# Two bottleneck blocks: filter sums in quarter pieces, eight plain products for the first two tiles, shared PSUM in the last stages

## The chip, the cores and the metric

One core of a Trainium2 chip. The metric is the device time of one execution in microseconds (us), as a median of several; the profile is one more execution under the hardware profiler. Runs of one kernel in one call differ by up to 0.4% (the kernel before: 2285.18 to 2294.29 us), and all runs used here are of the fast state.

## The reference, cut to what matters

Two blocks, one after the other, on x of 64 x 1024 x 14 x 14 (fp32). Each convolution is followed by a batch norm with the statistics of this very batch, so every stage must end before the next can scale anything.

```python
out = relu(bn(conv1x1(x,   w1, b1), g1, be1))    # 1024 -> 256 channels
out = relu(bn(conv3x3(out, w2, b2), g2, be2))    # 256 -> 256
out =      bn(conv1x1(out, w3, b3), g3, be3)     # 256 -> 1024
x   = relu(x + softplus(residual_scale) * out)
```

## The kernel before

It goes in stages, per block: conv1 (two tiles of 392 pixels at a time, seven products instead of eight, with sums of the halves on VectorE); conv2 (the 3x3 filter by transformed filters `u`, which must be computed from the taps first); the Gram stage, which transposes the normalised activations `y` and multiplies them with themselves, so that the statistics of conv3 come out without running conv3; conv3 with the residual, fused in block 0 with the next block's conv1.

The transformed filters of both blocks are built in the first stage, each half of a block's filters as one long run of VectorE instructions. Six results share two buffers, each free again only when its store to DRAM is done:

```python
def filters(b):
    for s in range(MS):
        spare = y_all[:, s, NPX // 2 - GPX :]
        ...
        for i in range(NF):
            u = part(15 * M + (i % 2) * NK * M, NK, M)         # two buffers in turn
            ...                                                # 768 elements at a time
            nc.vector.scalar_tensor_tensor(r, g[:, 1], by, base, ALU.mult, ALU.add)
            nc.vector.tensor_sub(u[:, D2], u[:, D3], u[:, D1D2])
            nc.vector.tensor_sub(u[:, D1], u[:, D0], u[:, D1D2])
            nc.gpsimd.dma_start(out=us[b][i][:, s], in_=u)
```

The weight sums for the seven products (the scheduler may move them; for the second block they landed in front of the first Gram stage):

```python
nc.vector.tensor_add(s[:, 0], a[1][0], a[1][1])
nc.vector.tensor_sub(s[:, 1], s[:, 0], a[0][0])
nc.vector.tensor_sub(s[:, 2], a[0][0], a[1][0])
nc.vector.tensor_sub(s[:, 3], a[0][1], s[:, 1])
```

The end of a Gram stage: six dense products, then the tiny ones, whose moving operand has two columns (`zmean`) or one (`ones`):

```python
for o in range(CS):
    for s in range(MS):
        nc.tensor.matmul(quad[:, o, 0:2], w3[:, s, o, :], m[:, s, :], ...)
for o in range(CS):
    for s in range(MS):
        nc.tensor.matmul(quad[:, o, 2:3], q[:, s, o * P : (o + 1) * P], ones, ...)
```

## Time and profile before

The median is 2287.72 us of 3 runs; the profiled execution has a span of 2286.1 us at a mean granted TensorE clock of 0.968 (the share of full speed that the profile shows).

| stage | from, to (us) | what to know |
|---|---|---|
| conv1, block 0, and all filters | 0 to 352.6 | five waits of TensorE for VectorE after the first load |
| conv2, block 0 | to 700.4 | 12.7 us at its start |
| Gram, block 0 | to 816.1 | 26.4 us at its start |
| statistics, conv3, residual, next conv1 | to 1469.6 | |
| conv2, block 1 | to 1817.0 | 12.7 us at its start |
| Gram, block 1, then conv3 and residual | to 2286.1 | 11 us at its start |

### The profile page before, as it was taken

The numbers are of one execution on the slowest core, as the hardware profiler recorded it, in microseconds if no ns is written. First come the engines' busy times: TensorE is split into PE (matmuls) and PEld (weight loads), VectorE is DVE, ScalarE is ACT, GpSimd is POOL, SyncE is SP. The second block draws the span as 40 slices with busy tenths as digits, with TensorE's granted clock in tenths as the row PEclk, the third lists the DMA queues.
The fourth block names the chain that finished last, engine by engine and source line by source line (L and its number), as shares of the span: only waits on it lengthen the run. The fifth ranks groups of instructions, "written<-read, shape, count | busy, mean of one in ns | idle before, by whom it ended". The sixth has DMA issues, their size and how long they took to land.

```text
span 2286.1 us, 22406 instructions
## 1 busy us (share of the span) xinstructions
PE 2164.1 (95%) x9008; PEld 1592.5 (70%) x9008; DVE 1357.5 (59%) x2086; ACT 571.0 (25%) x911; POOL 48.3 (2%) x102
## 2 busy tenths in 40 slices
PE   5989997999995999999999999799999899999997
PEld 2545556999994975555555555499999798555554
DVE  6765566887864345455555555577887633444443
ACT  1001115111113112323232232331111130444443
POOL 0000000000000000000000000000000000000000
PEclk8899998999997989999999999899999998999999
DMA  8765434555553014434434343345555410677874
GB/s 306 276 225 179 183 114 152 193 184 187 202 187 121 1 57 169 169 144 174 161 149 182 148 169 141 126 170 194 189 184 188 178 66 29 261 312 299 309 310 169
DMA packets 43016, 409.12 MB, mean 179 GB/s; under 512 B 4768, under 2 KB 5024, under 8 KB 9632
## 3 DMA queue, kind: packets, MB, share of 16 engines
q1 hardware_dynamic: 28800, 286.80, 34.4%
q0 software_dynamic: 12672, 118.49, 12.5%
q10 hardware_dynamic: 1440, 2.40, 0.3%
q8 instruction: 71, 1.16, 0.2%
q14 instruction: 33, 0.27, 0.0%
HBM read 289.18 MB, written 118.49 MB: 178 GB/s over the span
## 4 chain that ended last, share of the span: by engine, by line
PE 90%; issue 4%; DVE 2%; DMA 2%; ACT 1%; POOL 0%; ACTq 0%; POOLq 0%
PE ps L126 29%; PE bu L126 14%; PE bp L126 7%; PE ps L329 6%; PE ps L324 6%; PE ps L335 6%; PE ps L331 5%; PE ps L337 5%; PE ps L425 4%; PE bx L126 3%; PE ps L426 2%; PE ps L437 2%; DMA w<-in_w 1%; DMA u<-y 1%; PE ps L483 1%
## 5 line engine op out<-in xcount | busy, mean ns | idle before, releaser
L126 PE MATMUL ps<-y,w 128*128 128x392 f32 x2048 | 686.7, 495 | 0.6 <-DVE quad L485 0.3
L126 PEld LDWEIGHTS ps<-y,w 128*128 128x128 f32 x2048 | 391.1, 191 | 287.7 <-issue 4.4
L499 DVE SCALAR_TENSOR_TENSOR x<-ps,scale,x 128x392 f32<-128x392 f32 x512 | 317.1, 625 | 283.4 <-PE ps L126 279.1
L500 ACT ACTIVATE x<-x,shift 128x392 f32<-128x392 f32 x512 | 315.5, 622 | 442.4 <-DVE x L499 442.4
L126 PE MATMUL bu<-t,w1s 128*128 128x392 f32 x512 | 187.1, 510 | 29.4 <-DVE t L220 28.1
L357 DVE TENSOR_TENSOR f<-ps,ms 128x448 f32<-128x448 f32 x192 | 113.4, 602 | 147.2 <-PE ps L337 79.8
L324 PE MATMUL ps<-sums,u 128*128 128x224 f32 (+1 forms) x768 | 172.1, 347 | 25.4 <-DVE sums L304 12.7
L329 PE MATMUL ps<-r,u 128*128 128x224 f32 (+1 forms) x768 | 173.6, 347 | 0.0
L126 PEld LDWEIGHTS bu<-t,w1s 128*128 128x128 f32 x512 | 100.1, 197 | 105.5 <-DVE t L220 21.4
L335 PE MATMUL ps<-r,u 128*128 128x224 f32 (+1 forms) x768 | 172.1, 345 | 0.0
L324 PEld LDWEIGHTS ps<-sums,u 128*128 128x128 f32 x768 | 137.3, 190 | 26.8 <-issue 13.3
L331 PE MATMUL ps<-r,u 128*128 128x192 f32 (+1 forms) x768 | 153.8, 321 | 0.0
L337 PE MATMUL ps<-r,u 128*128 128x192 f32 (+1 forms) x768 | 153.3, 321 | 0.0
L189 ACT ACTIVATE u<-bu 128x392 f32<-128x392 f32 x96 | 47.7, 497 | 385.2 <-PE bu L126 385.2
L329 PEld LDWEIGHTS ps<-r,u 128*128 128x128 f32 x768 | 141.8, 190 | 1.3
L348 ACT ACTIVATE ms<-ps 128x448 f32<-128x448 f32 (+1 forms) x80 | 41.9, 524 | 390.7 <-PE ps L324 390.7
L335 PEld LDWEIGHTS ps<-r,u 128*128 128x128 f32 x768 | 136.0, 188 | 1.3
L439 DVE TENSOR_TENSOR zt<-ps,crow 128x512 f32<-128x512 f32 x98 | 67.8, 693 | 111.2 <-PE ps L437 111.2
L331 PEld LDWEIGHTS ps<-r,u 128*128 128x128 f32 x768 | 132.8, 189 | 1.1
L337 PEld LDWEIGHTS ps<-r,u 128*128 128x128 f32 x768 | 131.8, 188 | 1.0
L425 PE MATMUL ps<-zt 128*128 128x257 f32 x392 | 119.1, 385 | 0.5 <-DVE zt L439 0.5
L229 DVE TENSOR_TENSOR t<-x,t 128x1568 f32<-128x1568 f32 x32 | 57.3, 1792 | 84.2 <-PE bu L126 84.2
(125 smaller groups left out, 2163.3 us busy)
## 6 DMA issues: line engine op xcount, KB each, us to landing
u<-u SPq DMA_DIRECT2D x96, 1280.0 KB, 5.5
x<-in_x SPq DMA_DIRECT2D x62, 1568.0 KB, 6.6
mid<-x POOLq DMA_DIRECT2D x32, 1568.0 KB, 5.5
x<-mid SPq DMA_DIRECT2D x32, 1568.0 KB, 6.4
out<-x POOLq DMA_DIRECT2D x32, 1568.0 KB, 5.7
u<-y POOLq DMA_DIRECT2D x24, 640.0 KB, 6.9
y<-in_w SPq DMA_DIRECT2D x4, 1152.0 KB, 11.0
x<-in_x SPq DMA_DIRECT2D x4, 784.0 KB, 7.2
```

The costliest lines, as they stand in the source:

```text
L126: tc.keep_in_program_order(nc.tensor.matmul(*args, **kw))
L229: nc.vector.tensor_sub(self.v2, self.half[1][0], self.v2)
L324: nc.tensor.matmul(m[:, o, :n], w(s, D1D2), sums[:, s].rearrange("p l c -> p (l c)"), start=(s == 0), stop=(s == MS - 1),)
L329: nc.tensor.matmul(odd, w(s, D1), r[:, s, :, WH:], start=(s == 0), stop=False)
L331: nc.tensor.matmul(odd[:, :, : WH - 1], w(s, D3), r[:, s, :, WH + 1 :], start=False, stop=(s == MS - 1))
L335: nc.tensor.matmul(even, w(s, D2), r[:, s, :, :WH], start=(s == 0), stop=False)
L337: nc.tensor.matmul(even[:, :, 1:], w(s, D0), r[:, s, :, : WH - 1], start=False, stop=(s == MS - 1))
L357: nc.vector.tensor_tensor(f[:, o].rearrange("p r (i q c) -> p q (r i) c", i=GI, q=2)[:, :, :lines], eos[o][:, :, :n].rearrange("p q (l c) ...
L425: nc.tensor.matmul(g0, zt[:, c, 0:P], zt[:, c, :], start=first, stop=last)
L439: nc.vector.tensor_tensor(zt[:, :, :M], tp.rearrange("p (c m) -> p c m", c=CH), crow[:, None, :].to_broadcast([P, CH, M]), ALU.subtract,)
L499: nc.vector.scalar_tensor_tensor(v, ps, scale[:, o : o + 1], v, ALU.mult, ALU.add)
L500: nc.scalar.activation(v, v, AF.Relu, bias=shift[:, o : o + 1])
```

## The change

Its intent is to take the waits for VectorE out of the first stage and of the Gram start. The core of the diff, cut:

```diff
+        tc.keep_in_program_order(nc.vector.tensor_add(s[:, 0], a[1][0], a[1][1]))
...
+        tc.keep_in_program_order(nc.vector.tensor_sub(s[:, 2], a[0][0], a[1][0]))
...
-    def filters(b):
+    def filters(b, s, o, spare):                       # a quarter of a block's filters
+        nc.scalar.activation(even, even, AF.Copy, scale=-1.0 / 6)   # scalings to ScalarE
...
+            u = second[:, (i - 1) * n : i * n] if 0 < i < NF - 1 else first[...]   # own memory
...
+        for t, xt in enumerate(pair):
+            plain_conv1(psum, t, xt, w1[0], par[0], stats1)    # eight products, no sums
...
-            if t in (0, 6):
-                filters(t // 6)
+            if pieces and t % 4 == 2:
+                filters(0, *pieces.pop(0), spare)              # block 0, in the first stage
...
+            if k % 12 == 2 and beside:
+                beside.pop(0)()                                # block 1, in the Gram stage
...
-            with psum_pool() as psum:
+            with psum_pool(5) as psum:                         # shared with conv3 and conv1
+                made = [conv3(psum, 0, o, w3) for o in range(2)]   # ahead of the statistics
...
+            nc.vector.tensor_add(qs[0], qs[0], qs[1])          # halves the ones-products
```

The pieces in the Gram stage use the memory of the x tiles. The statistics' products are now kept in program order. PSUM stands for the buffers, called banks, that the products are written to. Not shown: the first and last term of each piece are now made by ScalarE, the two subtractions of a term are one instruction, and the four loads of a block's `w1` are issued in another order.

## The prediction

> **What bounds the kernel now.** I read the page first, then the sum of the waits of TensorE, then the order in time of the three places which that sum points at. The page says that TensorE is busy nearly all the time, and its row of slices says where it is not: slices 0 to 2 (57 us each), slice 6, slice 12, slice 25 and slice 31.
>
> ```profile
> PE 2164.1 (95%) x9008; PEld 1592.5 (70%) x9008; DVE 1357.5 (59%) x2086; ACT 571.0 (25%) x911; POOL 48.3 (2%) x102
> PE   5989997999995999999999999799999899999997
> ```
>
> The chain that ended last is 90% TensorE as well. So the time is TensorE's work plus TensorE's idle time, and a part of the change counts only if it removes one of the two. The sum of TensorE's waits gives the idle time by cause (us in total, times, longest):
>
> ```profile
> PE ps L437 <- ACT y L250: 39.1, 4, 26.4
> PE bu L126 <- DVE t L220: 28.1, 3, 12.2
> PE ps L324 <- DVE sums L304: 12.7, 1, 12.7
> PE ps L324 <- ACT t L264: 12.7, 1, 12.7
> PE bp L126 <- DVE y L198: 7.4, 2, 5.7
> PE bu L126 <- DMA w<-in_w: 7.0, 1, 7.0
> ```
>
> The L324 rows are the two starts of the 3x3 stage, which the change leaves alone. The L126 rows (42.5 us with the first load) all lie in the first stage, before 135 us. The TensorE timeline of that stretch (start, duration, then the idle time before it in brackets) shows a second cost beside each wait:
>
> ```profile
> 11.97 2.80 PE L126 MATMUL bx<-x,w 128*128 128x392 f32 x8
> 22.73 5.57 PE L126 MATMUL bu<-t,w1s 128*128 128x392 f32 x8 [7.96 <-DVE t L220]
> 56.51 5.59 PE L126 MATMUL bu<-t,w1s 128*128 128x392 f32 x8 [12.21 <-DVE t L220]
> 133.19 5.17 PE L126 MATMUL bu<-t,w1s 128*128 128x392 f32 x8 [7.91 <-DVE t L220]
> ```
>
> A product of eight instructions shows 2.80 us and follows the next after 2.63 us; after a long idle time it shows 5.2 to 5.6. VectorE is late because it builds the filters of both blocks here, in order with the sums that TensorE wants, and stands still when a filter buffer is still being stored:
>
> ```profile
> 126.11 0.96 DVE L156 SCALAR_TENSOR_TENSOR y<-y 128x768 f32<-128x768 f32 x1 [6.42 <-DMA u<-y]
> 131.35 1.78 DVE L220 TENSOR_TENSOR t<-t,x 128x1568 f32<-128x1568 f32 x1
> ```
>
> The 26.4 us wait is the start of the first Gram stage. VectorE's timeline there shows the weights of the next layer (L115, L113), which nobody needs for another 130 us, standing ahead of the few tiny instructions that make scale and shift:
>
> ```profile
> 705.65 1.89 DVE L512 BATCH_NORM_AGGREGATE mv<-stats 128x2 f32<-128x192 f32 x2
> 717.84 0.69 DVE L115 TENSOR_TENSOR w1s<-w 128x512 f32<-128x512 f32 x1 [10.31 <-DMA w<-in_w]
> 721.79 0.69 DVE L113 TENSOR_TENSOR w1s<-w 128x512 f32<-128x512 f32 x1 [3.10 <-DMA w<-in_w]
> 724.83 0.16 DVE L540 TENSOR_TENSOR shift<-shift,par 128x2 f32<-128x2 f32 x1
> ```
>
> In the second Gram stage, where no weights stand in between, aggregation ends at 1824.10 and the first normalisation starts at 1826.15: 2.05 us instead of 17.5.
>
> [...] after 7.9 to 12.2 us of idle time the product took 5.2 to 5.6 us, after a gap of 1.72 us (at 119.75) it took 2.90. [...] in slice 0 the kernel moved 306 GB/s, [...] I place them by their landing in this trace.
>
> **The change part by part.**
>
> 1. First stage. Removed: all five waits of L126 after the first load. Their idle time is 28.1 + 7.4 = 35.5 us. The stage ran from 7.04 to 352.6, which is 345.6 us, for 16 x 7 = 112 products x 2.633 = 294.9 us; so 50.7 us were lost, 35.5 idle and some 15 to slow products (about five at 2.5 to 2.9) and small gaps.
>    After: the first load lands as before (7.04). Tiles 0 and 1 take 8 plain products, which need no VectorE: 8 x 2.633 + 2.5 for the cold start = 23.6, so to 30.6. Their inputs are there: in the old trace the four halves of x land at 6.8, 9.4, 13.5 and 15.3, and the last is wanted after 20. Meanwhile tiles 2 and 3 land at 19 and 22.7 (issue at 9.6 and 10.0 plus 9.4 and 12.7), and VectorE needs 3 x 1.7 for their sums: ready at about 28, wanted at 35.8. Then 15 pairs x 7 x 2.633 = 276.5: end at 307.1 if nothing waits.
>    Does anything wait? Four pieces remain here, one in every second pair. A piece on VectorE is six instructions of 384 elements (0.48 us apart, between the old 256 at 0.34 and 768 at 0.87) and six of 256: 4.9 us. A pair has 18.4 us, and VectorE's usual work in it is 4 x 1.7 + 3 x 0.55 + 4 x 0.48 = 10.4 us, so it fits. Where the compiled order puts it (after the sums of the next pair, before the update of v2) it has 5 us to spare. Two places are tight: the first and last terms of pieces 3 and 4 wait for a fresh load of the taps, queued behind an x tile and the six stores of the piece before; I reckon it lands 11 to 13.5 us into a pair, and the copy that needs it stands on ScalarE ahead of u3, which TensorE wants at 13.2. I allow 1 us for all. Gain: 50.7 - 2.5 - 2.6 (one more product) - 1 = 44.6.
>
> 2. Start of the first Gram stage. The compiled order has the weights gone from between aggregation and shift; what stands before the first normalisation is 2.05 us, as in the second Gram stage. Gain 17.5 - 2.05 = 15.4. They come back at the start of the residual stage, part 4.
>
> 3. Pieces in the Gram stage. VectorE has room (0.69 of each 1.75 us), but a piece stands as one block of about nine instructions plus two waits for ScalarE's scalings (about 0.5 us each): 2 x 0.48 + 0.2 wait + 4 x 0.48 + 4 x 0.34 + 0.4 = 4.8 us. The compiled order lets TensorE run four groups of transposes ahead over the five banks. From the end of transpose group 14: products 13 (1.31), transposes 15 (0.44), products 14 (1.31), transposes 16 to 19 (1.76) make 4.82 us before TensorE wants zt 15; VectorE has zt 14 (0.65), the piece (4.8) and zt 15 (0.65), 6.1. So 1.3 us lost per piece, three times, and some 0.3 for the first, which is split around zt 3: loss 4.2. ScalarE's 16 normalisations at 1.6 us are done some 30 us in, just before the second piece.
>
> 4. End of both Gram stages. Adding the two halves of q on VectorE takes two instructions of 0.65 us, covered by 4.6 us of other products, and halves the products with ones: 16 of 32 instructions, 6.84 / 2 = 3.4 us. The two conv3 tiles in front cover the wait for g (0.3) and the gap before the residual (0.3), and work 2.63 us which is only moved. Gain 4.0 + 4.4 with the better first transposes. In block 0 the four weight instructions now stand between the first residual updates: VectorE is 2.6 us later, the free banks cover part, loss 1.5. Gain 6.9.
>
> Not moved: the 3x3 stages and the rest of the residual stages have the same order on each engine. One bank more or less for conv3, and bu = 1, change nothing where TensorE never waited for a bank.
>
> Sum: 44.6 + 15.4 - 4.2 + 6.9 = 62.7. 2287.7 - 62.7 = 2225.
>
> **The rivals.** First: the pieces hurt in the Gram stage, each gap being long enough to slow TensorE's clock, or VectorE waiting on ScalarE, which runs up to nine normalisations in a row. For it: a gap of 5.68 us did bring the slow clock back. Against it: I find gaps of 1.3, and 1.72 did not. If each piece cost 5 us the time would be 2241. Second: the first stage stays tied to transfers: [...] a late tap load delays u3, then TensorE. For it: the old kernel shows just such waits for stores. Against: the pieces now have their own memory, and the first reuse comes a whole pair later. If each of the four pieces cost 4 us there: 2240. Third: everything is hidden better than I think: no loss in the Gram stage and none in part 4, 2219.
>
> **Range and chances.** The gains 1 and 2 are idle time which the trace measures and the compiled order removes; the losses are worked out and small. One rival at full strength still leaves about 2240, both 2256. The 2% line is at 2242. Range 2215 to 2241. Faster by over 2%: 0.91; within 2%: 0.085; slower: 0.005.
>
> **What would show it.** The wait of L126 for L220 gone and the first stage over near 308; the gap before the first transposes of block 0 down from 26.4 to about 11; gaps of about 1.3 us four times in that Gram stage; the product with ones down to 3.4 us; 3x3 and last stages unchanged in length. It would be wrong if TensorE waits for u3 (L189) or a tap load in the first stage, or if products in the Gram stage show cold durations after the pieces.

The 2.5 us for the cold start is my estimate from the slow products of the trace (5.1 to 5.6 us where 2.80 is usual). With 768 elements, a scaling took 550 to 553 ns on VectorE and a sum 952, so the scalings that went to ScalarE were VectorE's cheap half. That loads before 30 us are near a limit was not shown.

## More of the kernel before

The next lines are the windows of the kernel before: from and to, length, busy time (and count) of PE (TensorE's products), PEld (its weight loads), DVE (VectorE), ACT (ScalarE) and POOL (GpSimd), then the granted clock of TensorE, the share of DMA and its GB/s. They are the first stage, the first Gram stage, and the statistics after each Gram stage.

```profile
0.00:352.56 352.56, 309.41 (x896) 175.76 (x896) 223.15 (x294) 37.69 (x71) 13.87 (x30) 0.94 0.57 208
700.41:816.05 115.64, 88.12 (x589) 81.69 (x588) 45.26 (x77) 25.68 (x17) 0.20 (x4) 0.88 0.16 61
816.05:833.46 17.41, 16.84 (x77) 13.88 (x76) 3.88 (x14) 0.28 (x1) 0.00 (x0) 0.72 0.00 0
1917.86:1934.63 16.77, 16.20 (x77) 13.24 (x76) 3.70 (x12) 0.28 (x1) 0.00 (x0) 0.75 0.00 1
```

Read the last two beside the first two. TensorE is busy for 16.84 of 17.41 us, yet the clock is 0.72: it was 1.00 from 811 to 823.8 us and 0.50 from 823.9 to 837.5, so here the half clock isn't the trail of an idle gap.

## The result, and the profile after

The changed kernel takes 2220.44 us (median of 4, 2219.34 to 2220.92) against 2288.50 (4 runs) before: a ratio of 0.9698, 95% interval 0.9681 to 0.9715. A ratio is the mean time of one kernel's runs over that of the other's of the same rounds, so not quite the ratio of the two medians. Faster by 3.0%, within the predicted range and 4.6 us below the predicted time. The profiled span went from 2286.1 to 2217.4 us, the mean clock from 0.968 to 0.985.

The page of the changed kernel, busy time and slices of TensorE:

```profile
PE 2144.0 (97%) x8984; PEld 1578.6 (71%) x8984; DVE 1343.1 (61%) x2091; ACT 585.8 (26%) x943; POOL 60.9 (3%) x126
PE   8999979999989999999999999799999799999997
```

Slice 0 shows 8 where it showed 5, slice 2 shows 9 where it showed 8; the 5 of slice 12 has become an 8, now in slice 11. The five largest of TensorE's waits (us in total, times, longest):

```profile
PE ps L451 <- ACT y L264: 22.4, 4, 11.0
PE ps L338 <- DVE sums L318: 12.7, 1, 12.7
PE ps L338 <- ACT t L278: 12.7, 1, 12.7
PE ps L126 <- DMA w<-in_w: 7.1, 1, 7.1
PE bx L439 <- DVE zt L453: 4.0, 4, 1.3
```

The 35.5 us of the first stage are gone, 39.1 at the Gram starts have become 22.4, and one row has grown, that for `zt` (0.5 us before, 4.0 now): VectorE is late four times with a transposed tile because a piece of filters stands before it. The same windows of the changed kernel as those shown of before:

```profile
0.00:308.08 308.08, 300.37 (x904) 172.70 (x904) 189.85 (x247) 45.78 (x87) 13.69 (x30) 1.00 0.56 205
656.06:760.20 104.14, 88.88 (x589) 81.81 (x590) 60.64 (x121) 33.13 (x33) 13.04 (x28) 0.95 0.46 166
760.20:773.34 13.14, 13.14 (x70) 9.16 (x68) 4.96 (x13) 0.28 (x1) 0.00 (x0) 0.98 0.00 0
1855.71:1868.70 12.99, 12.99 (x69) 9.01 (x68) 4.79 (x12) 0.28 (x1) 0.00 (x0) 0.99 0.01 1
```

From the ends of the stages on TensorE I made this account. "End of block 0" runs from the last Gram product to the first product of the next layer (816.05 to 856.63 before, 760.20 to 793.70 after); "end of block 1" from the last Gram product to TensorE's last instruction (1917.86 to 2274.63, 1855.71 to 2204.98).

| part | predicted gain | before, after (us) | gain in the traces |
|---|---|---|---|
| first stage | 44.6 | 352.56, 308.08 | 44.5 |
| first Gram stage, start and pieces | 15.4 - 4.2 = 11.2 | 115.64, 104.14 | 11.5 |
| ends of both Gram stages | 6.9 | 40.58 + 356.77, 33.50 + 349.27 | 14.6 |
| all the rest | 0 | | -1.9 |
| sum | 62.7 | 2286.1, 2217.4 | 68.7 |

The rest is conv2 of block 0 (0.1 longer), conv2 of block 1 (0.8) and the time after TensorE's last instruction (1.0). The 0.8 us are the clock: after the idle time at its start, conv2 of block 1 ran at half clock for 5.5 us (1419.29 to 1424.79), before for 3.8 (1482.22 to 1486.06). The 1.0 I didn't follow. Two terms hit. One was off by a factor of two, and the clock in the windows says where to look. The TensorE timeline there, of the kernel before (start, duration, count):

```profile
821.61 4.75 PE L480 MATMUL ps<-zmean,w 128*128 128x2 f32 x32
826.22 6.96 PE L483 MATMUL ps<-ones,q 128*128 128x1 f32 x32
833.46 23.34 PE L126 MATMUL ps<-y,w 128*128 128x392 f32 x64 [0.28 <-DVE ones L465]
856.63 2.80 PE L126 MATMUL bu<-x,w 128*128 128x392 f32 x8
```

and of the changed kernel:

```profile
767.83 3.63 PE L126 MATMUL bu<-zmean,w 128*128 128x2 f32 x32
771.32 2.16 PE L126 MATMUL bu<-ones,q 128*128 128x1 f32 x16
773.34 6.95 PE L126 MATMUL ps<-y,w 128*128 128x392 f32 x16
780.46 13.40 PE L126 MATMUL ps<-y,w 128*128 128x392 f32 x40 [0.16 <-DVE x L515]
793.70 2.80 PE L126 MATMUL bu<-x,w 128*128 128x392 f32 x8
```

An instruction with one column took 6.96 / 32 = 0.22 us before. After, it took 0.112 us from start to start while the clock was full (from the starts in the trace), and 2.02 / 16 = 0.126 over the whole group, whose last two ran at half clock. The dense ones after them were slow in both: 16 of them 6.95 us, where 16 x 0.329 = 5.3 is usual. Finer windows show when the clock changed. Before:

```profile
821.60:823.00 1.40, 1.40 (x15) 1.39 (x13) 0.69 (x1) 0.00 (x0) 0.00 (x0) 1.00 0.02 6
823.00:824.50 1.50, 1.50 (x13) 1.50 (x13) 0.00 (x0) 0.00 (x0) 0.00 (x0) 0.79 0.00 0
828.00:830.00 2.00, 2.00 (x11) 2.00 (x11) 0.00 (x0) 0.00 (x0) 0.00 (x0) 0.50 0.00 0
836.00:838.00 2.00, 2.00 (x5) 0.99 (x4) 0.90 (x3) 0.62 (x1) 0.00 (x0) 0.62 0.98 401
```

After:

```profile
769.50:771.30 1.80, 1.80 (x18) 1.80 (x18) 0.00 (x0) 0.00 (x0) 0.00 (x0) 1.00 0.00 0
771.30:773.30 2.00, 2.00 (x18) 2.00 (x18) 0.00 (x0) 0.00 (x0) 0.00 (x0) 0.89 0.00 0
775.00:777.00 2.00, 2.00 (x5) 1.09 (x5) 1.61 (x10) 0.00 (x0) 0.00 (x0) 0.68 0.76 295
```

TensorE has no gap (2.00 of 2.00 us busy), and still the clock goes to half some time into the tiny products. A share of, say, 0.79 in a window that mixes 1.0 and 0.5 gives the moment of the change. By such windows of a quarter us it was at half clock for 13.65 us in each block before and for 3.41 us after: 4 x 3.41 and 1 x 3.41. The clock records in the trace give the same lengths.

### The profile page after: what moved, and what is told of

Same layout as the page of the kernel before. It is cut to its first block, busy times and chain, and to the rows that moved or that the text cites. A ratio compares the mean times of both kernels' runs of the same rounds, so it can differ in the third digit from the quotient of the medians.

```text
span 2217.4 us, 22513 instructions
## 1 busy us (share of the span) xinstructions
PE 2144.0 (97%) x8984; PEld 1578.6 (71%) x8984; DVE 1343.1 (61%) x2091; ACT 585.8 (26%) x943; POOL 60.9 (3%) x126
## 4 chain that ended last, share of the span: by engine, by line
PE 83%; issue 12%; DVE 2%; ACT 1%; POOL 1%; DMA 1%; POOLq 0%; ACTq 0%; DVEq 0%; SPq 0%
PE ps L126 19%; PE bu L126 15%; PE bp L126 7%; PE ps L343 6%; PE ps L349 6%; PE ps L338 6%; PE ps L345 6%; PE ps L351 6%; PE bx L126 4%; PE bx L439 4%; PE bp L440 2%; PE ps L451 2%; ACT y L264 1%; POOL out L519 1%; DVE spare L155 0%
## 5 line engine op out<-in xcount | busy, mean ns | idle before, releaser
L338 PE MATMUL ps<-sums,u 128*128 128x224 f32 (+1 forms) x768 | 172.1, 347 | 25.4 <-DVE sums L318 12.7
L126 PE MATMUL bu<-t,w1s 128*128 128x392 f32 x496 | 173.6, 493 | 1.3 <-ACT u L189 1.3
L126 PEld LDWEIGHTS bu<-t,w1s 128*128 128x128 f32 x496 | 94.1, 190 | 71.0 <-ACT u L189 2.8
L439 PE MATMUL bx<-zt 128*128 128x257 f32 x392 | 119.3, 386 | 4.1 <-DVE zt L453 4.0
L264 ACT ACTIVATE y<-y,shift,scale 128x1568 f32<-128x1568 f32 x64 | 103.6, 1682 | 6.4 <-DVE shift L556 6.4
```

The lines of the kernel that those rows point to most:

```text
L126: tc.keep_in_program_order(nc.tensor.matmul(*args, **kw))
L264: nc.scalar.activation(y, y, AF.Relu, bias=shift[:, s : s + 1], scale=scale[:, s : s + 1])
L338: nc.tensor.matmul(m[:, o, :n], w(s, D1D2), sums[:, s].rearrange("p l c -> p (l c)"), start=(s == 0), stop=(s == MS - 1),)
L439: nc.tensor.matmul(g0, zt[:, c, 0:P], zt[:, c, :], start=first, stop=last)
```

## The experiments

Four groups, 12 kernels, all correct. Times stand against 2220.44 for the changed kernel. Differences of 1 or 2 us are read from the profile, stage by stage, not from the medians.

### What slows the end of the Gram stage

The tiles in front taken away:

```diff
-                made = [conv3(psum, 0, o, w3) for o in range(2)]
+                made = []
```

> The changed kernel with no tiles of the last convolution in front of the statistics products. Profile of the changed kernel: granted clock 1.0 until 5.1 us into the tiny products (one or two columns each), then 0.5 until 3.3 us later; before the change it fell 2.3 to 2.6 us into them and stayed at 0.5 for 14 us. Theory A (the number of tiny products in a row, that is the time spent in them, decides how long the array is at half clock; what stands in front of them only fills the 0.3 us wait for g): products with ones still about 2.0 to 2.4 us in the mean of the two blocks unless the clock happens to fall early, cold stretch under 8 us, +0.6 us per block for the two waits: +1 to +3 us in all (2221.5 to 2223.5). Theory B (the dense tiles in front keep the clock up): the clock falls within 2.6 us of the start of the tiny products in both blocks, ones-products 3.4 us, cold stretch of some 9 us, +4 to +7 us in all (2224.5 to 2227.5).

Measured: 2222.01 us. The clock fell 3.6 and 3.4 us after the first tiny product and stayed at half for 6.83 us, twice 3.41. Rival B wanted under 2.6 us and some 9; Theory A's bound of 8 holds, though its 2.0 to 2.4 us for the ones-products did not (3.5). The plainest word against B came from other runs: with the tiles in front, the clock also fell after 3.0 us (first block of the run with free weight sums) and after 3.5 (the run with spread pieces).

The two halves not added, 32 instructions with ones as before:

```diff
-            nc.vector.tensor_add(qs[0], qs[0], qs[1])
...
-            matmul(quad[:, o, 2:3], q[:, 0, o * P : (o + 1) * P], ones, start=True, stop=True)
+            for s in range(MS):
+                matmul(quad[:, o, 2:3], q[:, s, o * P : (o + 1) * P], ones, start=(s == 0), stop=(s == MS - 1))
```

> The changed kernel with the two halves of q not added: 32 instructions with ones (16 products) instead of 16, still in program order and with the two dense tiles in front. Theory A (time in tiny products decides): the clock falls some 2.5 to 5 us into them as in the changed kernel, the later part of the ones-products runs at 214 ns each: they take 5.5 to 6.9 us instead of 2.0, so +3.5 to +5 us per block, +7 to +10 in all (2227 to 2230), the cold stretch 8 us or longer. Theory B (dense tiles in front, or the fixed program order, keep the clock up): all 32 at 126 ns, 4.0 us, +2 per block, +4 in all (2224). My prediction had used 214 ns for each of those taken away, that is 3.4 per block, +6.8.

Measured: 2226.57 us, +6.1, a little under Theory A's 7 to 10 and above B's 4. TensorE in the first block:

```profile
768.91 3.63 PE L126 MATMUL bu<-zmean,w 128*128 128x2 f32 x32
772.40 5.45 PE L126 MATMUL bu<-ones,q 128*128 128x1 f32 x32
777.71 4.45 PE L126 MATMUL ps<-y,w 128*128 128x392 f32 x8
```

The clock fell 5.2 us in and was at half for 6.83 us instead of 3.41. So 16 more tiny instructions cost their own 16 x 0.112 = 1.8 us at full clock, and one more slow stretch of 3.41 us.

The dense tiles moved between the two kinds of tiny products:

```diff
         for o in range(CS):
             ... matmul(quad[:, o, 0:2], w3[:, s, o, :], m[:, s, :], ...)
+        made = [conv3(psum, 0, o, w3) for o in range(2)]
         for o in range(CS):
             matmul(quad[:, o, 2:3], q[:, 0, o * P : (o + 1) * P], ones, ...)
```

> The changed kernel with the two dense tiles of the last convolution (2.6 us) moved from in front of the statistics to between the 32 tiny products with zmean (3.5 us) and the 16 with ones (2.0 us). Same instructions, other order. Theory A (an uninterrupted stretch of tiny products counts as idleness for the clock): the dense tiles break the stretch, the clock does not fall or falls for one short stretch only, the first 16 instructions after the statistics take 5.4 us instead of 6.95; the wait for g (0.3) comes back: -1 us per block, -2 in all (2218.4). Theory C (the slow first tile of the last stage is due to the tiny VectorE work or the weights of the next layer there, not to the clock): 6.9 us as before, and +0.3 per block, +0.6 in all (2221).

Measured: 2218.95 us, -1.5; its profiled run was its slowest (2221.48), and its trace shows no gain: one stretch of 3.41 us per block again, which began 3.8 and 3.4 us after the first tiny product, on the dense tiles. 3.5 us of `zmean` alone were enough. In addition TensorE waited 0.6 and 0.8 us for the scale. A miss for Theory A as I had put it, and no support for Theory C, which had no clock in it: the clock fell here too. What it taught: 3.5 us of tiny products in a row were still too many.

### Where the pieces stand

Pieces of the Gram stage spread, one or two VectorE instructions at a step (their order fixed, by a generator):

```diff
-            if k % 12 == 2 and beside:
-                beside.pop(0)()
+            if k >= 2:
+                next(beside, None)
...
```

> The changed kernel with each piece in the Gram stage spread over nine steps of the loop instead of standing as one block of VectorE instructions. In the changed kernel TensorE waits for VectorE four times there, 4.0 us in all (1.27 us at pieces 2 to 4). Theory P (VectorE's block is longer than the four groups of transposes that run ahead): the waits vanish, at most 0.5 us is left, -3.5 to -4 us (2216.5). Theory Q (the waits are for ScalarE's scalings or for the load of the taps and come back whatever the order): 3 us or more of waits for zt remain, at more places, -1 to +1 us (2219.5 to 2221.5).

Measured: 2218.63 us, -1.8. Theory P holds: the row of waits for zt is gone, and the first Gram stage, from its first transpose, takes 88.2 us instead of 93.1. But fixing the order also moved a piece in the first stage, which ended 2.3 us later with a wait of 2.2 us for VectorE; that ate half of it. At the end of block 0 the clock was down for 6.83 instead of 3.41 us, which cost another 1.2.

Pieces of block 1 back in the first stage, one in each of seven pairs of tiles, one left in the Gram stage:

```diff
-            if pieces and t % 4 == 2:
+            if pieces and t < 16:
...
```

> The changed kernel with the pieces moved back from the Gram stage: seven of the eight in the first stage, one in every pair of tiles from the second to the eighth, and one left in the Gram stage. In the changed kernel each piece in the first stage after the first costs a wait of 0.6 us for u, and each in the Gram stage after the first one 1.27 us. Theory (VectorE has room in every pair: 10.4 + 4.9 of 18.4 us, so half of the pieces need not have gone to the Gram stage): three more waits of 0.6 in the first stage, 3.8 less in the Gram stage: -1 to -3 us (2217.5 to 2219.5); the pieces no longer keep the x tiles' memory, so the x tiles are fetched at the start of the Gram stage as in the kernel before. Rival (memory shared in turn by pieces in every pair makes each wait for the stores of the piece before, and the taps come late): TensorE idle 1 us or more at each, +3 to +10 us (2223 to 2230).

Measured: 2216.39 us, -4.1, more than expected. The first stage ended at 307.39 us, no later than with four pieces, and the waits for zt fell from 4.0 to 0.2 us, though at the end of each block the clock was down for 6.83 us instead of 3.41. So half of the pieces need not have gone to the Gram stage. My expectation had one thing wrong: the 0.6 us waits for u don't belong to the pieces (they stand near the ends of two stages, at 297 and 1397 us).

The results of a piece in two buffers in turn, as before, the size left:

```diff
-            u = second[:, (i - 1) * n : i * n] if 0 < i < NF - 1 else first[:, 3 * w :][...]
+            u = second[:, (i % 2) * n :]
```

> The changed kernel with the six results of a piece sharing two buffers in turn, as before, instead of memory of their own; the pieces stay quarters. Theory M (memory of its own was what took the waits for stores away): VectorE shows waits for stores of 2 us and more in the first stage again, TensorE 2 to 6 us of idle time in each of the four pairs with a piece and up to 4 us in the Gram stage per piece: +10 to +30 us (2230 to 2250). Rival S (the small size was what mattered: a store of a quarter is short and the scheduler puts other sums in between): under 5 us, 2220 to 2225.

Measured: 2222.96 us, +2.5 (its profiled run was its slowest, 2225.20); the first stage 5.0 us longer, where TensorE has four waits, of up to 1.2 us. Rival S is nearer in size, but the waits for stores did come back, by way of ScalarE. ScalarE, then VectorE, in the first pair with a piece:

```profile
66.93 0.52 ACT L152 ACTIVATE y<-y 128x384 f32<-128x384 f32 x1 [3.94 <-DMA u<-y]
```

```profile
67.48 0.43 DVE L156 TENSOR_TENSOR y<-y 128x256 f32<-128x256 f32 x1 [3.26 <-ACT y L152]
```

The scheduler has put the sums of the next tiles ahead of this part of the piece, so that TensorE feels little of the 3.26 us. Read these two lines with the changed kernel, where ScalarE also waits at this place, for fresh taps or a store, but in two pairs only (3.00 us at 63.17, 2.22 at 99.26; VectorE behind it 3.32 and 2.54). Here VectorE waits so in all four pairs, 3.1 to 3.7 us.

All four pieces of the first stage in one pair:

```diff
-            if pieces and t % 4 == 2:
+            while pieces and t == 2:
```

> The changed kernel with the four pieces of the first stage one after the other in one pair of tiles instead of one in every second pair; own memory kept (two places in turn). Theory (a piece costs VectorE 4.9 us, and there are some 5 to 8 us to spare ahead of the sums of the next pair): four pieces of 4.9 us are 20 us against 8 us to spare, so 10 to 16 us of idle time for TensorE in one place plus 2.8 us for the cold clock: +12 to +19 us (2232 to 2239). Rival (what hurt before was the wait for stores, not VectorE's own time): +3 us or less (2220 to 2223).

Measured: 2237.92 us, +17.5. TensorE, then VectorE in that place:

```profile
78.48 5.28 PE L126 MATMUL bu<-t,w 128*128 128x392 f32 x8 [13.55 <-DVE t L229]
```

```profile
65.96 0.56 DVE L139 TENSOR_TENSOR y<-y 128x384 f32<-128x384 f32 x1 [3.22 <-DMA u<-y]
76.56 1.77 DVE L229 TENSOR_TENSOR t<-x,t 128x1568 f32<-128x1568 f32 x1
```

One wait of 13.55 us and one slow product, as the theory had it; VectorE waited 3.2 and 0.4 us for stores in it and worked the rest. Of the two means of the change in this stage, small pieces far apart bring more than own memory, 16.2 us against 5.0 at the end of the stage.

The first two tiles by seven products again:

```diff
-        for t, xt in enumerate(pair):
-            plain_conv1(psum, t, xt, w1[0], par[0], stats1)
...
-        now = start(2)
+        now = start(0)
```

> The changed kernel with the first two tiles done by seven products with sums, as the kernel before did. Theory (the idle time of 8.0 us at 22 us and the slow product after it come from the sums that wait for both tiles, whatever the filters do): the wait of the first t-product comes back with 7 to 9 us, a cold product +2.6 to 2.9, one product less -2.6: first stage ends 7 to 9 us later, 2228 to 2229. Rival (the early waits came from VectorE being held by the filters, which now start a pair later): under 3 us, 2220 to 2223.

Measured: 2225.31 us, +4.9; the first stage ended at 313.43 instead of 308.08:

```profile
21.10 4.39 PE L126 MATMUL bu<-t,w1s 128*128 128x392 f32 x8 [6.77 <-DVE t L220]
```

6.77 of waiting and 1.6 of slow clock, less one product of 2.63, make 5.7 for the measured 5.4. That is between the two expectations: the wait came back nearly as large as the theory had it (7 to 9), while the slow clock cost 1.6 and not 2.6 to 2.9.

### The start of the first Gram stage

The order of the weight sums left to the scheduler in the changed kernel, and, the other way round, fixed in the kernel before (the same two lines each):

```diff
-        tc.keep_in_program_order(nc.vector.tensor_add(s[:, 0], a[1][0], a[1][1]))
+        nc.vector.tensor_add(s[:, 0], a[1][0], a[1][1])
```

> The changed kernel without the fixed place of the weight sums of the next layer: they stand again between aggregation and shift at the start of the first Gram stage, where they wait for the load of w. Theory (the 15.4 us of that gap were the place of these four instructions): TensorE's gap at that start goes from 11.0 back to about 26 us, and the 0.2 us wait at the start of the last stage goes away: +15 us (2235). Rival (the loads of w come earlier or later now that the filter stores and taps are elsewhere, so the gap depends on the transfers): a gap of 13 to 20 us, +2 to +9 us (2222 to 2229).

> The kernel before with one part of the change alone: the weight sums of the next layer kept in program order. It also gives two more looks at the old statistics products (32 with zmean, 32 with ones, not kept in order). For the gap at the start of the first Gram stage (26.4 us before, 11.0 in the changed kernel, 18.2 in the changed kernel without the kept order). Theory (the order alone does it; the earlier landing of w in the changed kernel, where no x tiles are fetched at the same time, only matters without the kept order): gap 11.0 us, -15.4 us there, +1 to +2 at the start of the last stage: 2273.5 to 2275. Rival (both are needed): gap of 18 us or so, 2281. For the clock, Theory A [...]: the fall comes between 2.0 and 5.4 us after the first tiny product, and the cold stretch is again a whole number of 3.41 us, 3 or 4 times. Theory B2 (the old order makes it fall early): 2.2 to 3.0 us in both blocks.

Measured: 2228.55 us for the first, +8.1 where the theory said 15 (its profiled run was its slowest, 2230.99): the gap before the first transposes was 18.2 us, the rival's. For the second, 2270.31 us against 2288.22 (ratio 0.9926, 0.9911 to 0.9941); the gap was 11.0, 15.4 us less. The median lies below the theory's 2273.5 to 2275, whose loss of 1 to 2 us at the start of the last stage didn't come (40.6 us at the end of block 0 in both). VectorE in the first run:

```profile
666.38 0.69 DVE L115 TENSOR_TENSOR w1s<-w 128x512 f32<-128x512 f32 x1 [3.49 <-DMA w<-in_w]
```

It waits 3.49 us for w where the kernel before waited 10.31. Part of that is the new order of the four loads, since L115 now needs the second of them and not the third; but the sums can't end before the last, and that landed 21.4 us after the end of conv2 before and 13.0 here. Between the end of conv2 and the normalisation the kernel before moved 6.92 MB (three x tiles among it), this one 3.61 MB: the pieces hold the x tiles' memory, so no x is fetched then and w lands sooner. That the missing x loads are the reason is my reading; no run changes them alone. The DMA engines were busy throughout there in the kernel before (share near 1):

```profile
708.00:712.00 4.00, 0.00 (x0) 0.00 (x0) 0.00 (x0) 0.00 (x0) 0.00 (x0) 0.50 0.99 410
712.00:716.00 4.00, 0.00 (x0) 0.00 (x0) 0.00 (x0) 0.00 (x0) 0.00 (x0) 0.50 1.04 435
```

So two parts of the change each take away some of this gap, and their gains don't add: the kept order alone brings all of it (15.4 us), the rest of the change without the kept order about half (8.2).

The second run also gave two more looks at the old statistics: the clock fell 3.1 and 3.2 us in, again for 13.65 us. That is just inside Theory A's range and just at the edge of B2's, so it doesn't part them.

### Both repairs together

Spread pieces with the order fixed in the Gram stage alone, and four dense tiles, one in front of the tiny products and three among them, two of these in the banks of g0 and g1:

```diff
...
             ... matmul(quad[:, o, 0:2], w3[:, s, o, :], m[:, s, :], ...)
+            if o in (2, 5):
+                made.append(conv3(psum, 0, len(made) + 1, w3, tag="bx" if o == 2 else "bp", bufs=1))
...
             matmul(quad[:, o, 2:3], q[:, 0, o * P : (o + 1) * P], ones, start=True, stop=True)
+            if o == 1:
+                made.append(conv3(psum, 0, len(made) + 1, w3))
```

> The changed kernel with two additions: the pieces of the Gram stage spread over its steps as in the run before, their order fixed only there (fixing it in the first stage too had cost 2.2 us there), and four dense tiles of the last convolution set between the tiny products, two of them in banks that are free by then, so that no more than 1.5 us of tiny products stand in a row. Spread: waits for zt in the Gram stage 4.0 us to under 0.5, that stage 4 to 5 us shorter. Mixed, Theory A [...]: the clock stays at 1.0 in both blocks and 1.5 to 2 us are saved in each unless TensorE then waits for scale and shift (up to 0.8 us). In all -5.5 to -8.5: 2212 to 2215. Rival C (the slow stretch is not a matter of their share in a window): the clock falls to 0.5 as before, nothing saved at the ends, 2215.5 to 2216.5.

Measured: 2211.93 us (2210.88 to 2212.49), -8.5, ratio to before 0.9667. TensorE in the first block, then the windows of the two ends with their clock:

```profile
762.32 1.40 PE L126 MATMUL bu<-zmean,w 128*128 128x2 f32 x12
763.58 1.56 PE L126 MATMUL bx<-y,w 128*128 128x392 f32 x4
764.98 1.40 PE L126 MATMUL bu<-zmean,w 128*128 128x2 f32 x12
...
779.44 10.77 PE L126 MATMUL ps<-y,w 128*128 128x392 f32 x32 [1.85 <-DVE x L527]
```

```profile
756.01:771.55 15.54, 15.54 (x78) 10.45 (x76) 4.96 (x13) 0.28 (x1) 0.00 (x0) 1.00 0.00 1
1850.49:1866.02 15.53, 15.53 (x76) 10.44 (x76) 4.79 (x12) 0.28 (x1) 0.00 (x0) 1.00 0.01 1
```

The clock never leaves 1.00. Rival C falls. In the first block TensorE now outruns VectorE, which has the four weight sums between the first residual updates: waits of 0.29 and 1.85 us.

By stages, most of the gain is the spreading: the first Gram stage, from its first transpose, takes 88.2 us instead of 93.1. The full clock shows at the end of block 1 (1.5 us shorter); at the end of block 0 the new waits ate it (34.0 us instead of 33.5). The profiled span fell by 6.7 us in all.

The weight sums moved into the end of the Gram stage:

```diff
-                w1 = combine_w1(one, b + 1, w1)
+                w1 = later[0]          # made step by step after the pieces, beside the Gram products
...
```

> The best kernel so far (2211.93 us) with the weight sums of the next layer moved out of the start of the last stage into the end of the first Gram stage, one or two instructions at a step. In the best kernel TensorE, now at full clock there, waits 1.85 + 0.29 us for VectorE in the first block, where those four instructions (2.6 us) stand between the first residual updates; in the second block, which has none, it doesn't wait. Theory (these waits are the four instructions): they fall to under 0.3 us, the end of the first Gram stage stays free of waits, -1.8 to -2.1 us (2209.5 to 2210.5). Rival (the wait is the chain of tiny instructions before scale and shift, and the weights only stand in its shadow): no change, 2211.5 to 2212.5.

Measured: 2211.75 us (5 runs, 2209.89 to 2212.03). The waits are gone, and from the last Gram product to the next layer's first product it is 31.6 us instead of 34.0. So the theory's cause holds and its time doesn't: hardly anything came of it. The trace shows where it went: conv2 of block 1 started 2.3 us earlier (1413.34 instead of 1415.64), but after its 12.7 us of idle time the clock came back at 1419.1 and 1419.0 us in the two kernels. The start of that conv2 in the run before and in this one:

```profile
1415.64:1419.00 3.36, 3.36 (x9) 3.07 (x10) 3.36 (x5) 3.36 (x5) 0.00 (x0) 0.50 0.03 7
1413.34:1419.10 5.76, 5.76 (x16) 5.35 (x17) 5.76 (x10) 5.76 (x6) 0.00 (x0) 0.50 0.01 3
```

So the 2.3 us were run at half clock, and 1.1 us were left at the end of that stage. After the next idle time, at the start of the second Gram stage, 0.5 us were left at the end of that stage (1849.97 instead of 1850.49), and the spans differ by 0.5.

## Why the prediction was right or wrong

**First stage, 44.6: right, 44.5.** The waits for L220 are gone, and the end near 308 came out. The four pieces together (+16.2 us at the end of this stage), seven products (+5.4) and shared buffers (+5.0) show what each part holds back; they make 26.6 of the 44.5. The rest has no run of its own: none puts the long instructions or VectorE's scalings back. That the term hit to 0.1 us is luck: of the 1 us that I had set aside for late loads, 0.64 went to a wait for `u` at 297 instead. The copy on ScalarE that I called tight did wait 3.0 us for its taps (at 63.17) and its like in the next piece 2.2 us for a store (at 99.26), with no wait of TensorE there.

**Gram start, 15.4: right, by a cause with two halves.** The gap fell from 26.4 to 11.0, and the kept order alone does this. I had not seen that without it the gap would have shrunk to 18.2 as well.

**Pieces in the Gram stage, -4.2: right.** 4.0 us of waits, the longest 1.27 where I had 1.3; spread out they vanish.

**Ends of both Gram stages, 6.9: too small, 14.6.** This is the step that failed in size. Of the 14.6 us, 7.1 lie in block 0 and 7.5 in block 1. The halving of the ones-products was sized at 3.4 per block, and undoing it cost 3.4 us in block 1 and 3.0 in block 0; but that is luck, since 16 of them take 1.8 us at full clock and the rest was one slow stretch more. The rest of the step, "The two conv3 tiles in front cover the wait for g (0.3) and the gap before the residual (0.3)", left out the clock. I took 6.84 us for 32 instructions as their nature; it was their time at half clock (0.213 us each, against 0.112 at full clock). The end of block 1, which all kernels but for this have in common, shows the term cleanly (times worked out as in the account above; the run with the tiles in between is left out, since it also waits 0.3 us for g there: one stretch, 349.82):

| kernels | slow stretches of 3.41 us | end of block 1 (us) |
|---|---|---|
| before, and before with kept order | 4 | 356.77, 356.77 |
| 32 ones-products | 2 | 352.69 |
| no tiles in front | 2 | 351.46 |
| two buffers; free sums; seven slots | 2 | 350.94, 350.93, 350.94 |
| changed; spread; seven products; together | 1 | 349.27, 349.27, 349.28, 349.28 |
| the two best | 0 | 347.79, 347.80 |

One stretch costs 1.5 to 1.7 us, half of its length. From 4 to 1 that is an estimated 3 x 1.7 = 5.1; 16 instructions at 0.112 are 1.8, and the two covered waits 0.6: 7.5, as measured.

Also in this step, "loss 1.5" for the weight sums in block 0: TensorE waited 0.16 us only, since it was itself slow there. At full clock the loss was 2.1, as the best kernel shows, and without the sums 0.

When the clock changes can be read from the traces. In the kernel before and in the changed kernel the clock records show 21 and 13 changes, each a whole number of steps of 3.413 us after the first, to within 0.01 us (1868.52 - 772.85 = 1095.67 us in the changed kernel is 321.0 x 3.413). In the runs with spread pieces and with seven slots, followed in windows of a quarter us, the two falls lie 322.0 and 321.0 such steps apart. Counted from the start of the span, the points of this grid lie differently in each of the four. At the eight ends of Gram stages of these four runs I added up the tiny products between one point of the grid and the next. At full clock, up to 1.95 us of them were followed by full clock (6 times), 2.27 us or more by half clock (8 times). At half clock, 0.49 us or less of them were followed by full clock (8 times), 1.15 or more by half clock (9 times). The fall came 2.3 to 5.4 us after the first tiny product, according to its place on the grid. This is a count over runs made for other ends: I made no run which shifts the products alone, and why tiny products count as they do stays open.

## What to carry to other kernels

A busy TensorE isn't a fast one (clock 0.50 with 2.00 of 2.00 us busy): read the granted clock beside the busy time, and don't size a removed instruction by a duration that was measured at half clock. Here 3.5 us of tiny products in a row sufficed to bring the half clock; with dense work set among them, so that no more than about 1.5 us of them stood together, the clock stayed at 1.00. Keep work that others wait for in small pieces, and spread it; a fixed order can also put a piece in a worse place, as in the first stage (2.2 us), so look where it lands. Gains from two parts that remove the same wait don't add, and a gain ahead of an idle gap can be half lost to the slow clock after it (2.3 us became 1.1 and then 0.5).
